# One kernel, seven small moves in its hand-written order: the first job in two token halves, weight sums on another engine, earlier preparation, expert weights in smaller parts

## The chip, the core and the metric

The kernel runs on one core of a Trainium2 chip. The metric is the time on the device in microseconds (us), lower is better. The core has five engines that matter here: TensorE (PE in the profile) for matrix products, VectorE (DVE) and GpSimd (POOL) for elementwise work, ScalarE (ACT) for activations and for copies out of the matmul banks, and SyncE (SP), which issues most DMAs. Each engine runs its own instructions in program order and waits for others by semaphores.

## What is computed

8192 tokens of 512 features, fp32. Cut to what matters:

```python
xn = layernorm(x)
h, f, i = split(xn @ W1 + b1, 3)              # 512 -> 3 x 1024
# gates from f and i in log space, value from h, then a scan along the sequence
hidden = scan(coefficient(f, i), value(h), init_h)
s = hidden @ W2 + b2                           # 1024 -> 512
shared = (silu(xn @ gate) * (xn @ up)) @ down  # 512 -> 1024 -> 512
e = argmax(xn @ gate_w)                        # one of 32 experts per token
routed = swiglu_e(xn * sigmoid(max logit))     # 512 -> 1024 -> 512, weights of expert e
out = x + s * silu(shared + routed)
```

## The kernel before

**Two halves.** The first half (up to about 2820 us) walks over the tokens in 16 chunks of 512 and does the recurrence and the shared expert. The second walks over the 32 routed experts: it gathers each expert's tokens by a table, multiplies, and adds the result to what the first half left in DRAM.

**Jobs and slots.** A chunk has 20 jobs, each one pair of 128-column blocks of one weight (h, f, i of the recurrence, g and u of the shared expert), 512 features by 256 columns. A job has 7 slots, a chunk 140 (`SC`). The loop over slots at the end of the file emits, for each slot, one piece of TensorE's work and then whatever was registered for this slot with `at(slot, function, ...)`. Nothing reorders it: the order in which the program is written is the order on every engine, so each `at` is a place in the queues of the engines that the function uses. What waits in a queue holds up all that stands behind it there.

**Chunk 0 and the others.** Chunk 0 multiplies plainly (`plain`, L641): per job two blocks of four accumulating matmuls of 128x512, evicted by ACT at the last (L661, L663) from three rotating banks `b`. Chunks 1 to 15 use a seven-product scheme (`multiply`, L665): each job has products P1 to P7 of 128x256, which need sums of weight blocks and of token blocks. The weight sums are made in chunk 0 (`combine`, L573: POOL L585 and L589, DVE L587 and L591), saved to DRAM and fetched later; the sums of token blocks (`t_sum`, L612, DVE L626) are made at the start of each chunk. The products' evicted parts are joined by additions (L720), on DVE or POOL.

**Preparation.** `Prep` loads a chunk's four token tiles, normalises them (L417), transposes them, makes the router's logits (L467 to L477), takes the largest (L485 to L497) and scales the tokens for the experts (`scale`, L506). `Prep.plan` places each of these steps in the chunk ahead of the one that it serves; for chunk 1 everything is shifted by 50 slots. Chunk 0's own preparation is the head of the program: four transposes per token tile on TensorE (L455), a copy each by ACT (L458), then the vector of biases (L1278) and the first job.

**Cells.** A `Cell` is the gate arithmetic of one pair of blocks: m = min(f, i, 0) on DVE (`low`, L758), f and i less m on POOL (`less`, L762), three exponentials on ACT (L766), f and i with m added on POOL (`weigh`, L771), their sum and its reciprocal on DVE (L775, L778, two halves), value, products (L792 to L782) and the scan (L804). Its steps stand at fixed slots behind the job of f, in `Cell.plan`.

**Projection.** The second products (W2, shared down) use the seven-product scheme too: `out_sum` (L878) makes four sums of weight blocks for each of the two, 128x1024 each (L886), and stores them to DRAM (`tdram`). `project_out` emits units of eight matmuls (L981), with weights `wP` that SP fetches in 512 KB tiles; in chunks 1 to 15 its units lie between the jobs' products, and the last chunk's units come at the end of the first half, alone.

**The table.** Each token's rank within its expert is counted chunk by chunk (`Dispatch.ranks`). After chunk 14, `places` computes on 32 partitions where each expert's tokens go: a chain of small DVE operations (L1099 to L1127) that ends in a matmul (`terms`, L1131). The token numbers are then written into a table in DRAM, merged, read back (`two`, `table`, `number`: L1239 to L1261), and turned into row addresses (`fours`, L1262), by which POOL gathers the tokens of the first experts (L205, L212) and their rows of the first half's results (`e_rest`, L222). The generator that makes the table does one part per slot; a bare `yield` in it lets a slot pass.

**The passage to the experts.** While the last units run, SP also fetches expert 0's weights: gate ahead of the loop, up in its 6th step, down in its 26th, 2 MB each (`weight`, L186).

Of the kernel before, what the change touches and what calls it, by code (L numbers as in the profile page):

```python
# [8 lines left out]
FP = mybir.dt.float32  # L9
# [8 lines left out]
P = 128  # L18
T = 512
# [14 lines left out]
def tile_kernel(  # L34
# [135 lines left out]
    class Chunk:  # L170
# [12 lines left out]
                (t, min(P, width - t * P)) for t in range(-(-width // P))  # L183
            ]

        def weight(self, tag):  # L186
            q = "gud".index(tag)
            w = self.alloc_w([P, KH * I], f"{self.name}_w{tag}")
            w = w.rearrange("p (k f) -> p k f", k=(KH, KH, NI)[q])
            self.src = self.src or self.w_src()  # L190
            rows = "(k p) f -> p k f" if tag == "d" else "(p k) f -> p k f"
            nc.sync.dma_start(out=w, in_=self.src[q].rearrange(rows, p=P))
            self.wt.append(w)

        def weights(self):
            for tag in "gud":
# [178 lines left out]
    def at(slot, what, *args):  # L375
        assert slot >= now
        steps.setdefault(slot, []).append(lambda: what(*args))
# [3 lines left out]
    class Prep:  # L381
# [126 lines left out]

        def plan(self, g):

            g += 50 if self.c == 1 else 0
            for t in range(NT):
                at(g + 2 + 2 * t, self.load, t)
                at(g + 16 + 2 * t, self.stats, t)
                at(g + 32 + 2 * t, self.normal, t)
                at(g + 35 + 2 * t, self.store, t)
                at(g + 43 + 2 * t, self.pieces, t)
                at(g + 50 + 2 * t, self.turn, t)
                at(g + 72 + 2 * t, self.again, t)
                at(g + 86 + t, self.scale, t)  # L520
            at(g + 12, self.keep)
            at(g + 24, self.variance, 0, NT)
            at(g + 28, self.spread, 0, NT)
            at(g + 66, self.router)
            at(g + 72, self.logits)
            at(g + 76, self.choose)
            at(g + 80, self.score)
# [113 lines left out]
    def bias(n, block):  # L641
        p, kind = JOBS[n % JC]
        col = "hfi".index(kind) * NJ + 2 * p + block
        return vec[:, col : col + 1]

    def plain(n, s):

        kind = JOBS[n % JC][1]
        for m in (s, s + 1) if s == 6 else (s,):
            block, k = divmod(m, KH)  # L650
            if k == 0:
                banks[n, block] = ps_b.tile([P, 512], FP, tag="b", name=f"b{block}_{n}")
            ps = banks[n, block]
            nc.tensor.matmul(
                ps, lhsT=natural[n][:, k, block * P : (block + 1) * P], rhs=xnTs[0][:, k, :],
                start=(k == 0), stop=(k == KH - 1),
            )
            if k == KH - 1:
                o = outs[n] if block else out_of(n)
                if kind in "gu":  # L660
                    nc.scalar.copy(o[:, block, :], ps)  # L661
                else:
                    nc.scalar.activation(o[:, block, :], ps, AF.Identity, bias=bias(n, block))  # L663

    def multiply(name, n):  # L665

        c = n // JC
        kind = JOBS[n % JC][1]
        A11, A12, A21, A22 = blocks(n)
        S = sums.get(n)  # L670
        b = xnTs[c]

        def B(k, m):
            return b[:, k * KQ : (k + 1) * KQ, m * HT : (m + 1) * HT]

        lhs, rhs, bank = {
            "P1": lambda: (A11, B(0, 0), "b"),
            "P2": lambda: (A12, B(1, 0), "a"),
            "P3": lambda: (S[:, 3], B(1, 1), "c"),
            "P4": lambda: (A22, tsum[c, 4], "b"),  # L680
            "P5": lambda: (S[:, 0], tsum[c, 1], "c"),
            "P6": lambda: (S[:, 1], tsum[c, 2], "b"),
            "P7": lambda: (S[:, 2], tsum[c, 3], "b"),
        }[name]()
        new = name in ("P1", "P2", "P5")
        if new:
            if bank == "b":
                ps = ps_b.tile([P, 512], FP, tag="b", name=f"b{n}")
            else:
                ps = ps_x.tile([P, 512], FP, tag=f"x{(n + (bank == 'a')) % 2}", name=f"{bank}{n}")  # L690
            banks[n, bank] = ps
        ps = banks[n, bank][:, :HT]
        for k in range(KQ):
            nc.tensor.matmul(  # L694
                ps, lhsT=lhs[:, k, :], rhs=rhs[:, k, :],
                start=(new and k == 0), stop=(k == KQ - 1),

                skip_group_check=True,
            )

        def part(tag, bufs):
            o = jp.tile([P, HT], FP, tag=tag, name=f"{tag}{n}", bufs=bufs)
            outs[n, tag] = o
            return o

        def evict(o, block):
            if block is None or kind in "gu":
                nc.scalar.copy(o, ps)  # L708
            else:
                nc.scalar.activation(o, ps, AF.Identity, bias=bias(n, block))  # L710

        if name == "P1":
            out_of(n)
            evict(part("p1", 2), 0)
            return
        o = outs[n]

        def join(eng, out, *tags):
            l, r = (outs.pop((n, tag)) for tag in tags)
            at(now + 1, lambda: eng.tensor_tensor(out, l, r, ALU.add))  # L720

        if name == "P2":
            evict(part("a", 2), None)
            join(nc.vector, o[:, 0, :HT], "a", "p1")
        elif name == "P5":
            evict(part("p5", 2), None)
        elif name == "P6":
            evict(part("u2", 2), 0)
        elif name == "P3":
            evict(part("c", 2), None)  # L730
            join(nc.vector, o[:, 0, HT:], "c", "u2")
        elif name == "P7":
            evict(part("u3", 2), 1)
            join(nc.vector if c == NCHUNK - 1 else nc.gpsimd, o[:, 1, HT:], "u3", "p5")
        elif name == "P4":
            evict(o[:, 1, :HT], 1)
            natural.pop(n)
# [6 lines left out]
    class Cell:  # L744
# [66 lines left out]
        def plan(self):  # L811
            g = SC * self.c + 7 * JOBS.index((self.p, "f"))
            for slot, what, *args in (
                (24, self.low), (25, self.less, "f"), (25, self.less, "i"),
                (27, self.exp, "m"), (29, self.exp, "f"), (31, self.exp, "i"),
                (32, self.weigh, "f"), (33, self.weigh, "i"), (37, self.total),
                (38, self.invert, 0), (39, self.sigmoid), (40, self.positive),
                (41, self.invert, 1), (43, self.value), (44, self.weighed),
                (45, self.divide, "f"), (46, self.divide, "i"),
                (47, self.scan, 0), (48, self.scan, 1),  # L820
            ):
                at(g + slot, what, *args)

    class Hidden:
# [54 lines left out]
    def out_sum(half, q):  # L879
        B11, B12, B21, B22 = out_blks[half][:4]  # L880
        l, r = {
            1: lambda: (B12, B11), 3: lambda: (B22, B12),
            2: lambda: (B22, out_blks[half][4]), 4: lambda: (B21, out_blks[half][5]),
        }[q]()
        o = out_tile(f"ot{half}_{q}")
        nc.vector.tensor_tensor(o, l, r, ALU.subtract)  # L886
        if q in (1, 2):
            out_blks[half].append(o)
        d = tdram[half, q] = dram.tile([P, NP * HC], FP, name=f"tdram{half}_{q}")
        at(now + 3, lambda: nc.sync.dma_start(out=d[:, :], in_=o.rearrange("p q f -> p (q f)")))  # L890
# [121 lines left out]
    class Dispatch:  # L1012
# [69 lines left out]
        def places(self):  # L1082
# [42 lines left out]
                    terms[:, q * E : (q + 1) * E], of, by[:E, 0:1], None, ALU.mult  # L1125
                )
            nc.vector.tensor_copy(terms[:, 4 * E :], extra)  # L1127
            for _ in range(4):
                yield
            ps = work("terms")  # L1130
            nc.tensor.matmul(  # L1131
# [136 lines left out]
    for t in range(NT):  # L1268
        first.stats(t)
        first.variance(t, 1)  # L1270
        first.spread(t, 1)
        if t:
            first.normal(t - 1)
            first.transpose(t - 1)
    first.normal(NT - 1)
    first.transpose(NT - 1)
    vps = work("vps")
# [27 lines left out]
    def spread_out(gen):  # L1305
        if next(gen, gen) is not gen:
            at(now + 1, spread_out, gen)

    at(SC + 100, d.clear)
    for q in range(NCHUNK // GC - 1):  # L1310
        at(SC * (GC * (q + 1) - 2) + 94, lambda q=q: spread_out(d.ranks(q)))
    last = SC * (NCHUNK - 1)

    def table():
# [10 lines left out]
        for half in range(2):  # L1325
            at(max(end + 20, END + 4) + half, d.numbers, half)

    at(last - SC + 94, lambda: spread_out(table()))

    fill = project_out()  # L1330
    PER = len(UNIT) * NP * 2
# [42 lines left out]
    ps_w = ctx.enter_context(  # L1374
        tc.tile_pool(name="ps_w", bufs=4, space=PSUM, side="right", reuse_waits="tile")
    )
    chunks[0].weight("g")
    k = 0
    while filled < 2 * NCHUNK * PER:
        now += 1  # L1380
        for step in steps.pop(now, ()):
            step()
        while filled < due(now):
            next(fill)
            filled += 1
        k += 1
        if k in (6, 26):
            chunks[0].weight("ud"[k // 26])
    next(fill, None)
    while steps:  # L1390
        now += 1
# [93 lines left out]
```

## Time and profile before

| | |
|---|---|
| time, median of 3 runs | 4345.41 us (4343.04 to 4348.74) |
| the profiled execution | 4345.11 us |
| its span | 4343.3 us |
| instructions | 52,479 |
| DMA traffic | 889.58 MB, mean 205 GB/s |

The page divides the span into 40 slices (some 109 us each) and gives for each the busy share of every engine in tenths. Further views give, for an engine, the us that it waited for each releaser, and a timeline: start, duration, engine, line, operation, output and inputs with shapes, and in brackets the idle time ahead of it with what ended it. The costliest groups of the first half are the job products (L694: 618.9 us for `b<-t,sums` alone) and the projection's products (L981: 601.9 us); those of the second half are L261 and L272 (515 to 519 us each). The mean granted TensorE clock of the execution is 0.992.

### The profile page before, as it was taken

To read this page: it belongs to the slowest core of one execution; us is meant where nothing else is said; L and a number is where in the kernel's file an instruction comes from. 1 tells how busy PE (TensorE), PEld (TensorE's weight loads), DVE (VectorE), ACT (ScalarE), POOL (GpSimd) and SP (SyncE) were. 2 spreads that over 40 slices of the span, in tenths; PEclk is the share of its full clock that TensorE was granted. 3 is DMA by queue.
4 is the path that set the end of the run, shared out by engine and by line. 5 is a ranking of instruction groups with operands and counts; after the bars stand their busy time and mean duration, and the time that the engine had idled before them with its cause. 6 is when DMAs were issued, how large, how long until landed. Compare 5 with 4: busy or idle time off the path is not lost. (4 is left out here: it accounts for less than half of the span.)

```text
span 4343.3 us, 52479 instructions
## 1 busy us (share of the span) xinstructions
PE 4262.1 (98%) x19031; PEld 3560.0 (82%) x19031; DVE 2761.5 (64%) x3507; ACT 1661.3 (38%) x3319; POOL 1748.4 (40%) x1410
## 2 busy tenths in 40 slices
PE   8899999999999999999999999999999999999998
PEld 3488888888888888888888888866777788889998
DVE  6787877886977778778878788723334334343332
ACT  3355555555555555555555544401111111111111
POOL 4445444534453444445434536642222233332210
PEclk9999999999999999999999999999999999999999
DMA  7667676676666666766766655574555555565561
GB/s 245 204 213 225 213 222 208 207 230 206 212 213 223 219 209 209 224 202 214 223 217 214 209 187 169 183 255 165 185 185 183 177 213 201 197 230 204 205 230 63
DMA packets 459433, 889.58 MB, mean 205 GB/s; under 512 B 35167, under 2 KB 285823, under 8 KB 450980
## 3 DMA queue, kind: packets, MB, share of 16 engines
q1 hardware_dynamic: 431588, 796.22, 55.1%
q0 software_dynamic: 27584, 89.98, 6.5%
q8 instruction: 152, 2.49, 0.2%
q14 instruction: 109, 0.89, 0.1%
HBM read 787.64 MB, written 116.50 MB: 208 GB/s over the span
## 5 line engine op out<-in xcount | busy, mean ns | idle before, releaser
L694 PE MATMUL b<-t,sums 128*128 128x256 f32 x2400 | 618.9, 380 | 8.6 <-DVE t L626 6.3
L981 PE MATMUL u<-wP,s 128*128 128x256 f32 x2048 | 601.9, 381 | 2.4 <-DMA wP<-tdram 2.4
L261 PE MATMUL e_acc<-e_h,e_wd 128*128 128x296 f32 (+15 forms) x2048 | 515.4, 397 | 5.5 <-DVE e_h L280 5.5
L272 PE MATMUL e_g<-e_xsT,e_wg 128*128 128x296 f32 (+15 forms) x2048 | 518.7, 396 | 1.0 <-DVE e_xsT L242 1.0
L272 PE MATMUL e_u<-e_xsT,e_wu 128*128 128x296 f32 (+15 forms) x2048 | 518.0, 396 | 0.0
L694 PEld LDWEIGHTS b<-t,sums 128*128 128x128 f32 x2400 | 454.1, 190 | 75.4 <-issue 6.5
L212 POOL DMA_INDIRECT e_xs<-rec,fours x276 | 263.1, 953 | 553.3 <-DVE e_xsT L247 458.7
L261 PEld LDWEIGHTS e_acc<-e_h,e_wd 128*128 128x128 f32 x2048 | 390.0, 191 | 94.0 <-DVE e_h L280 6.1
L272 PEld LDWEIGHTS e_u<-e_xsT,e_wu 128*128 128x128 f32 x2048 | 389.0, 190 | 87.2
L272 PEld LDWEIGHTS e_g<-e_xsT,e_wg 128*128 128x128 f32 x2048 | 383.0, 190 | 81.9 <-DVE e_xsT L242 1.2
L981 PEld LDWEIGHTS u<-wP,s 128*128 128x128 f32 x2048 | 390.5, 191 | 57.8 <-issue 4.7
L778 DVE RECIPROCAL d<-d 128x512 f32<-128x512 f32 x128 | 427.8, 3344 | 1.6
L277 ACT ACTIVATE e_sig<-e_g 128x280 f32<-128x280 f32 (+15 forms) x256 | 102.6, 401 | 769.5 <-PE e_g L272 764.5
L279 DVE TENSOR_TENSOR e_sig<-e_sig,e_g 128x280 f32<-128x280 f32 (+15 forms) x256 | 112.1, 438 | 425.0 <-ACT e_sig L277 424.9
L762 POOL TENSOR_TENSOR f<-m,f 128x1024 f32<-128x1024 f32 x64 | 154.8, 2419 | 410.6 <-DVE m L758 321.7
L694 PE MATMUL c<-t,sums 128*128 128x256 f32 x1200 | 309.0, 380 | 6.4 <-DVE t L626 6.4
L694 PE MATMUL c<-xnT,sums 128*128 128x256 f32 x1200 | 310.1, 381 | 0.3
L694 PE MATMUL a<-xnT,nat 128*128 128x256 f32 x1200 | 309.7, 381 | 0.0
L694 PE MATMUL b<-xnT,nat 128*128 128x256 f32 x1200 | 308.0, 379 | 0.0
L694 PE MATMUL b<-t,nat 128*128 128x256 f32 x1200 | 308.0, 379 | 0.0
L694 PEld LDWEIGHTS c<-t,sums 128*128 128x128 f32 x1200 | 228.4, 190 | 37.9 <-DVE t L626 6.8
L694 PEld LDWEIGHTS c<-xnT,sums 128*128 128x128 f32 x1200 | 227.1, 190 | 37.1 <-ACT p L708 6.3
(237 smaller groups left out, 7185.8 us busy)
## 6 DMA issues: line engine op xcount, KB each, us to landing
sums<-sdram SPq DMA_DIRECT2D x300, 512.0 KB, 4.8
nat<-in_L_attn_W_dram SPq DMA_DIRECT2D x192, 512.0 KB, 4.4
wP<-tdram SPq DMA_DIRECT2D x128, 512.0 KB, 4.1
e_wg<-L_ffn_routed_gate_w_dram SPq DMA_DIRECT2D x32, 2048.0 KB, 15.5
e_wu<-n_L_ffn_routed_up_w_dram SPq DMA_DIRECT2D x32, 2048.0 KB, 8.2
e_wd<-L_ffn_routed_down_w_dram SPq DMA_DIRECT2D x32, 2048.0 KB, 13.7
nat<-L_ffn_shared_gate_w_dram SPq DMA_DIRECT2D x64, 512.0 KB, 4.6
nat<-n_L_ffn_shared_up_w_dram SPq DMA_DIRECT2D x64, 512.0 KB, 4.2
```

The source lines that it names most:

```text
L212: nc.gpsimd.indirect_dma_start(out=r[:, b, :], out_offset=None, in_=rec1.rearrange("n (a d) -> (n a) d", a=NA), in_offset=bass.IndirectOff ...
L261: nc.tensor.matmul(accs[m][:, :W], lhsT=wd[:, j, m * P : (m + 1) * P], rhs=h[:, :W], start=(j == 0), stop=(j == NI - 1),)
L272: nc.tensor.matmul(o[:, :W], lhsT=w[:, k, j * P : (j + 1) * P], rhs=xsT[:, k, :W], start=(k == 0), stop=(k == KH - 1),)
L277: nc.scalar.activation(sig[:, :W], g[:, :W], AF.Sigmoid)
L279: nc.vector.tensor_tensor(sig[:, :W], sig[:, :W], g[:, :W], ALU.mult)
L694: nc.tensor.matmul(ps, lhsT=lhs[:, k, :], rhs=rhs[:, k, :], start=(new and k == 0), stop=(k == KQ - 1),  skip_group_check=True,)
L762: nc.gpsimd.tensor_tensor(v, self.m, v, ALU.subtract)
L778: nc.vector.reciprocal(self.d[:, s, :], self.d[:, s, :])
L981: nc.tensor.matmul(ps[:, q, :], lhsT=lhs[:, q * P : (q + 1) * P], rhs=w[:, p, :],  start=(q == 0 and p == 0 and name in ("P1", "P2", "P5") ...
```

## The change

Seven edits, none of which changes what is computed:

1. `first_half` emits the first job's matmuls for the first 256 tokens (both blocks, eight of 128x256) after the second token tile's transposes and ahead of the third's; `plain` then does the second 256 tokens of that job only.
2. The eight subtractions of `out_sum` go from DVE to POOL.
3. Chunk 1's preparation stands 12 slots earlier (shift 38 rather than 50), and `scale` of every chunk four slots earlier.
4. In chunk 0, the steps of a cell in its slots 27 to 33 (the exponentials and the two additions of m) stand two slots later.
5. For the last jobs of chunk 14 (12 to 19) the join behind P2 goes from DVE to POOL.
6. The ranks, and with the last of them the table, begin 5 slots earlier; the table's generator lets 9 slots pass ahead of the `terms` matmul rather than 4.
7. Expert 0's weights are fetched in twelve parts of 512 KB, in every second step of the loop over the last units (four parts of gate, four of up, four of down), rather than in three DMAs of 2 MB.

```diff
@@ -183,14 +183,15 @@
                 (t, min(P, width - t * P)) for t in range(-(-width // P))
             ]
 
-        def weight(self, tag):
+        def weight(self, tag, part=slice(None)):
             q = "gud".index(tag)
-            w = self.alloc_w([P, KH * I], f"{self.name}_w{tag}")
-            w = w.rearrange("p (k f) -> p k f", k=(KH, KH, NI)[q])
+            if len(self.wt) == q:
+                w = self.alloc_w([P, KH * I], f"{self.name}_w{tag}")
+                self.wt.append(w.rearrange("p (k f) -> p k f", k=(KH, KH, NI)[q]))
             self.src = self.src or self.w_src()
             rows = "(k p) f -> p k f" if tag == "d" else "(p k) f -> p k f"
-            nc.sync.dma_start(out=w, in_=self.src[q].rearrange(rows, p=P))
-            self.wt.append(w)
+            src = self.src[q].rearrange(rows, p=P)
+            nc.sync.dma_start(out=self.wt[q][:, part, :], in_=src[:, part, :])
 
         def weights(self):
             for tag in "gud":
@@ -508,7 +509,7 @@
 
         def plan(self, g):
 
-            g += 50 if self.c == 1 else 0
+            g += 38 if self.c == 1 else 0
             for t in range(NT):
                 at(g + 2 + 2 * t, self.load, t)
                 at(g + 16 + 2 * t, self.stats, t)
@@ -517,7 +518,7 @@
                 at(g + 43 + 2 * t, self.pieces, t)
                 at(g + 50 + 2 * t, self.turn, t)
                 at(g + 72 + 2 * t, self.again, t)
-                at(g + 86 + t, self.scale, t)
+                at(g + 82 + t, self.scale, t)
             at(g + 12, self.keep)
             at(g + 24, self.variance, 0, NT)
             at(g + 28, self.spread, 0, NT)
@@ -648,12 +649,13 @@
         kind = JOBS[n % JC][1]
         for m in (s, s + 1) if s == 6 else (s,):
             block, k = divmod(m, KH)
-            if k == 0:
+            if k == 0 and n:
                 banks[n, block] = ps_b.tile([P, 512], FP, tag="b", name=f"b{block}_{n}")
             ps = banks[n, block]
+            part = slice(0 if n else HT, T)
             nc.tensor.matmul(
-                ps, lhsT=natural[n][:, k, block * P : (block + 1) * P], rhs=xnTs[0][:, k, :],
-                start=(k == 0), stop=(k == KH - 1),
+                ps[:, part], lhsT=natural[n][:, k, block * P : (block + 1) * P],
+                rhs=xnTs[0][:, k, part], start=(k == 0), stop=(k == KH - 1),
             )
             if k == KH - 1:
                 o = outs[n] if block else out_of(n)
@@ -661,6 +663,15 @@
                     nc.scalar.copy(o[:, block, :], ps)
                 else:
                     nc.scalar.activation(o[:, block, :], ps, AF.Identity, bias=bias(n, block))
+
+    def first_half():
+        for block in range(2):
+            ps = banks[0, block] = ps_b.tile([P, 512], FP, tag="b", name=f"b{block}_0")
+            for k in range(KH):
+                nc.tensor.matmul(
+                    ps[:, :HT], lhsT=natural[0][:, k, block * P : (block + 1) * P],
+                    rhs=xnTs[0][:, k, :HT], start=(k == 0), stop=(k == KH - 1),
+                )
 
     def multiply(name, n):
 
@@ -721,7 +732,9 @@
 
         if name == "P2":
             evict(part("a", 2), None)
-            join(nc.vector, o[:, 0, :HT], "a", "p1")
+
+            late = n // JC == NCHUNK - 2 and n % JC > 11
+            join(nc.gpsimd if late else nc.vector, o[:, 0, :HT], "a", "p1")
         elif name == "P5":
             evict(part("p5", 2), None)
         elif name == "P6":
@@ -819,6 +832,8 @@
                 (45, self.divide, "f"), (46, self.divide, "i"),
                 (47, self.scan, 0), (48, self.scan, 1),
             ):
+                if self.c == 0 and 26 < slot < 34:
+                    slot += 2
                 at(g + slot, what, *args)
 
     class Hidden:
@@ -883,7 +898,7 @@
             2: lambda: (B22, out_blks[half][4]), 4: lambda: (B21, out_blks[half][5]),
         }[q]()
         o = out_tile(f"ot{half}_{q}")
-        nc.vector.tensor_tensor(o, l, r, ALU.subtract)
+        nc.gpsimd.tensor_tensor(o, l, r, ALU.subtract)
         if q in (1, 2):
             out_blks[half].append(o)
         d = tdram[half, q] = dram.tile([P, NP * HC], FP, name=f"tdram{half}_{q}")
@@ -1125,7 +1140,7 @@
                     terms[:, q * E : (q + 1) * E], of, by[:E, 0:1], None, ALU.mult
                 )
             nc.vector.tensor_copy(terms[:, 4 * E :], extra)
-            for _ in range(4):
+            for _ in range(9):
                 yield
             ps = work("terms")
             nc.tensor.matmul(
@@ -1272,6 +1287,8 @@
         if t:
             first.normal(t - 1)
             first.transpose(t - 1)
+        if t == 2:
+            first_half()
     first.normal(NT - 1)
     first.transpose(NT - 1)
     vps = work("vps")
@@ -1308,7 +1325,7 @@
 
     at(SC + 100, d.clear)
     for q in range(NCHUNK // GC - 1):
-        at(SC * (GC * (q + 1) - 2) + 94, lambda q=q: spread_out(d.ranks(q)))
+        at(SC * (GC * (q + 1) - 2) + 89, lambda q=q: spread_out(d.ranks(q)))
     last = SC * (NCHUNK - 1)
 
     def table():
@@ -1325,7 +1342,7 @@
         for half in range(2):
             at(max(end + 20, END + 4) + half, d.numbers, half)
 
-    at(last - SC + 94, lambda: spread_out(table()))
+    at(last - SC + 89, lambda: spread_out(table()))
 
     fill = project_out()
     PER = len(UNIT) * NP * 2
@@ -1374,7 +1391,6 @@
     ps_w = ctx.enter_context(
         tc.tile_pool(name="ps_w", bufs=4, space=PSUM, side="right", reuse_waits="tile")
     )
-    chunks[0].weight("g")
     k = 0
     while filled < 2 * NCHUNK * PER:
         now += 1
@@ -1383,9 +1399,11 @@
         while filled < due(now):
             next(fill)
             filled += 1
+        if k % 2 == 0 and k < 24:
+            q, part = divmod(k // 2, 4)
+            part *= (1, 1, 2)[q]
+            chunks[0].weight("gud"[q], slice(part, part + (1, 1, 2)[q]))
         k += 1
-        if k in (6, 26):
-            chunks[0].weight("ud"[k // 26])
     next(fill, None)
     while steps:
         now += 1
```

## Prediction

> **What bounds it now.** I read the page first, then TensorE's waits, then the timelines of the engines around each wait. Times are of one profiled execution: 4345.1 us, of which the span is 4343.3; the runs shown have their median at 4345.4, so a sum made against the execution holds for the median to 0.3 us.
>
> ```profile
> PE 4262.1 (98%) x19031; PEld 3560.0 (82%) x19031; DVE 2761.5 (64%) x3507; ACT 1661.3 (38%) x3319; POOL 1748.4 (40%) x1410
> PE   8899999999999999999999999999999999999998
> PEclk9999999999999999999999999999999999999999
> ```
>
> TensorE is busy 98% of the span. No edit removes a matmul, so all that can be won is idle time and the slow clock behind it. The list of what TensorE waited for shows where:
>
> ```profile
> PE b L654 <- ACT u L661: 10.7, 2, 5.7
> PE terms L1131 <- DVE terms L1127: 6.5, 1, 6.5
> PE c L694 <- DVE t L626: 6.4, 1, 6.4
> PE b L694 <- DVE t L626: 6.3, 3, 3.8
> PE e_acc L261 <- DVE e_h L280: 5.5, 1, 5.5
> PE u L981 <- DMA wP<-L_ffn_shared_down_w_dram: 4.2, 1, 4.2
> PE lgp L467 <- DVE xnT L436: 3.7, 1, 3.7
> PE u L981 <- DMA wP<-tdram: 2.4, 1, 2.4
> ```
>
> Columns: waiting line, releaser, us in all, times, longest. By the timeline the waits are: chunk 0 at 81.1 (5.74), 102.3 (1.52), 124.7 (4.96), 152.8 (3.71); the start of chunk 1 at 186.7 (6.43), 192.4 (0.53), 200.3 (2.02); the table's terms at 2582.1 (6.49); chunk 15 at 2620.5 (3.79); the passage to the experts at 2815.5 (4.23), 2826.7 (2.40), 2848.3 (0.98), 2871.7 (5.52); with three small ones 51.8 us. After 2872 there is none, so nothing is to be had in the expert half.
>
> A long wait costs more than itself. Windows of the timeline (us, busy and count by engine, granted clock, DMA):
>
> ```profile
> 81.10:83.00 1.90, 1.86 (x2) 0.83 (x3) 1.87 (x5) 1.90 (x3) 0.00 (x0) 0.50 0.00 0
> 2582.05:2584.00 1.95, 1.95 (x7) 1.53 (x8) 0.18 (x1) 0.00 (x0) 0.00 (x0) 0.50 0.00 0
> ```
>
> Clock 0.50 lasts about 4 us behind a wait of 3.8 us or more (81.1 to 85.0, 2582.1 to 2586.0), which halves the work done: some 2 us each, seven times, 14 us. The upper bound of everything is 51.8 + 14 = 66 us.
>
> **VectorE against GpSimd.** The second thing to see is that the two hold one another up:
>
> ```profile
> 72.03 3.27 POOL L762 TENSOR_TENSOR f<-m,f 128x1024 f32<-128x1024 f32 x1 [2.63 <-DVE m L758]
> 73.01 3.37 DVE L782 TENSOR_TENSOR i<-i,d 128x1024 f32<-128x1024 f32 x1
> 81.14 19.67 PE L654 MATMUL b<-xnT,nat 128*128 128x512 f32 x40 [5.74 <-ACT u L661]
> ```
>
> POOL's subtraction takes 3.27 where it takes 2.35 with VectorE idle; VectorE's product, 1.21 elsewhere, takes 3.37. The wait at 81.14 is this chain's end: m on DVE, two subtractions on POOL to 78.57, exp m and exp f on ACT, and only then the eviction that frees TensorE's bank.
>
> **The change, part by part** (gain positive).
>
> *First job in halves.* Token tile 1 is in SBUF at 9.36 (ACT's copy, 8.77 + 0.59); the first matmul now starts at 12.91. So 16 matmul instructions of 128x256 can start at 9.4; at the cold 0.427 us they end at 16.2, warm from 13.9 on (as now, 4.4 us after the first) at 15.1. But the transposes of tiles 2 and 3 stand behind them on TensorE (now at 9.06), and from there to the vector transpose, two transposes and two copies, take 3.85 now. After 15.1 + 3.1 the other half, 12 instructions ahead of the router's matmul, lands at 20.6; now that is 20.48. Gain 0, from -2 to +1.
>
> *Chunk 0: the eight weight sums on POOL, exp two slots later, chunk 1's preparation 12 slots earlier.* A sum is 1.21 on DVE, 2.35 on POOL: DVE is relieved of 9.7 us, POOL gets 18.8. What counts is POOL's order. In the changed program two sums (2.35 each) and a job's 0.73 stand ahead of weigh f and weigh i of the first cell, and its less ops start 0.7 to 1.5 later: weigh i ends at 55.0 + 0.9 + 4.7 + 0.7 = 61.3. Behind it on DVE stand total, two reciprocals (3.34 each), value and the next cell's m: 70.7 becomes about 75.5, since one sum between them (1.2) is gone. The wait now at 81.14 then ends near 85.0: +4.8, less the exp f (0.96) that the eviction is now ahead of. The second cell: two sums again, weigh i at 95.5 instead of 89.6, the 102.3 wait ends near 108. Then it comes back: DVE idles for POOL or others now at 43 (4.30), 50 (6.15), 85 (5.23), 120, 127 (2.9 each), 160 (5.5), and the preparation of chunk 1 (normals, transposes, top-1, four scalings of 0.47) fills these holes rather than standing ahead of the token sums. The router wait (3.71) goes; the 124.7 wait ends near 128; the first token sum, bound by the reciprocals behind the last weigh, about 1.2 later than now; the third 0.8 earlier, because two scalings no longer precede it. Gain 0.8. Bounds: nothing comes back, -12 (6.3 and 5.9 both arrive at TensorE); all seven waits vanish, 24.9 + 3 x 2 = 31. I take the value by the rows of POOL's order, with -6 to +12 for the range.
>
> The Trainium skill, "GPSIMD Engine Reference", section "Engine selection", advises VectorE and not GpSimd for two-input elementwise work, about twice as slow. The rows' ratio agrees (2.35 to 1.21); by the rule alone the move would be a loss of 8 x 1.14 = 9 us, but it says nothing of which engine has idle time here.
>
> *Chunks 1 to 13.* Scalings four slots earlier, behind the score that they need; no wait is listed there now. 0.
>
> *Terms and chunk 15.* The table's chain on DVE runs from 2569.61 to 2581.90. Five of its operations on 32x1 or 32x32 take 2.0 to 2.3 us beside POOL's subtractions and additions (2567.05 to 2580.84), where their neighbours take 0.15 to 0.7. Five slots earlier (1.2 us each) it starts near 2564.5; most of it runs ahead of POOL and ends near 2568 to 2570, the eight joins moved to POOL (0.42 off DVE each) helping. The matmul keeps its slot, so the wait of 6.49 and its cold clock (2.4: 0.50 to 2586, 0.59 to 2588) go: 8.9. Behind it the last cell's m and weigh come 2.4 to 2.9 later; DVE's 6.31 idle us at 2582, in which it waited for the stalled TensorE, take that up, yet chunk 15's token sums, on a DVE without holes from 2588 on, give back about 1.4: 7.5. Bounds 3 (the sums give back all that DVE's hole gave) and 11 (the 3.79 at 2620 shrinks too).
>
> *Expert 0's weights in 512 KB parts.* The queue rows now:
>
> ```profile
> 2814.09 0.33 SPq L1254 DMA_DIRECT2D table<-two  x1
> 2828.22 3.79 SPq L1261 DMA_DIRECT2D number<-table  x8
> 2856.02 0.95 POOL L222 DMA_INDIRECT e_rest<-rec,idx  x1 [0.30 <-issue]
> 2866.12 0.69 DVE L297 TENSOR_TENSOR e_rest<-e_rest,b2b 128x512 f32<-128x512 f32 x1 [11.90 <-DMA e_rest<-rec,idx]
> ```
>
> 4 MB of expert weights stand ahead of the table's 93 KB (14.1 us to land) and of the wP tiles; in the changed order 3 MB do, spread, and wP's first two wait behind 0.5 and 1 MB rather than 2. The waits of 4.23 and 2.40 and a cold clock (2) can go. But the same bytes move, at 371 to 432 GB/s in these windows: about 466 would be needed to hide all, so some 6 of 8.6 remain as gain at the first expert's start. The table lands near 2818, so the gathers can start 8 us earlier; POOL's program order keeps part of that: an output join of the last unit (its matmuls end near 2831) stands second behind expert 1's first gather, and 23 gathers at 1.25 us follow before e_rest. That issue moves from 2856 to about 2861, while DVE has the e_rest addition ahead of the product that the 5.52 wait is for (2871.74). So that wait stays or grows, and e_acc starts 3 to 5 earlier. Gain 4, bounds 0 and 9. No row has expert weights in parts; the nearest is wP, 512 KB in 4.1 us median, 9.0 when queued.
>
> The skill's "DMA: Bandwidth & Descriptors", section "Rules for kernel authors", asks for at least 1 MiB per DMA and speaks against this part. By its measured table (341 GB/s at 1 MB, 425 at 16 MB) 6 MB would take 3.6 us longer, an estimate; the windows with 512 KB tiles among them show up to 432, so I count nothing.
>
> **Sum**: 0 + 0.8 + 0 + 7.5 + 4 = 12.3; 4345.1 - 12.3 = 4333.
>
> **Rivals.** *A, the waits mostly vanish* (4290 to 4324): chunk 0's holes on DVE take all, the passage hides wP and the gate on e_rest. 20 from chunk 0, 11 and 9: 40, to 4305. For it: most of DVE's time in chunk 0 is waiting; against: the chain m, less, weigh, total is what the waits end on, and POOL is in it. *B, slower: POOL's queue.* The sums ahead of weigh delay two cells by 6.3 and 5.9, nothing comes back, and e_rest's later issue eats the passage's gain: -12.2 - 2 for a cold restart, -5 at e_rest, +7.5: 4345.1 + 11.7 = 4357. It decides if weigh i of the first cell ends later than 61 and the wait at 124.7 doesn't shrink. *C, no change:* chunk 0 costs 6 to 8, terms give 7.5, the passage 0 to 4: 4337 to 4354, centre 4343. For it: two of the three gains hang on engines that stay in program order.
>
> **Chances.** Forecast (4324 to 4337) 0.50, A 0.16, C 0.26, B 0.08. About 0.2%, 8.7 us, is what a measurement can tell: faster 0.66, same 0.26, slower 0.08. The range 4310 to 4348 leaves out B and half of A, and holds chunk 0's -6 as well as its +12.
>
> **To look at in the changed profile.** terms should no longer wait; the router neither; the first two waits of chunk 0 should be near 85 and 108, with weigh i of the first cell ending near 61; the table's DMA lands near 2818, e_rest is issued near 2861, e_acc starts near 2867 less what was won before. I'm wrong if weigh i is not late (then A), or if chunk 1 starts more than 5 us later than now (then B or C).

## The result

The changed kernel takes 4346.23 us (median of 12 runs, 4344.56 to 4348.44) against 4345.05 us for the one before (12 runs beside it): a ratio of 1.0004, 95% interval 0.9995 to 1.0013. That is no change. The profiled execution has a span of 4345.3 us against 4343.3.

The page's busy line, after:

```profile
PE 4261.2 (98%) x19047; PEld 3561.2 (82%) x19047; DVE 2803.5 (65%) x3491; ACT 1662.5 (38%) x3319; POOL 1767.0 (41%) x1426
```

TensorE's waits, after (line, releaser, us in all, times, longest; the lines of the file have moved by 1 to 15):

```profile
PE b L656 <- ACT u L663: 12.0, 3, 8.0
PE e_acc L262 <- DVE e_h L281: 7.7, 1, 7.7
...
PE b L705 <- DVE t L627: 6.4, 4, 3.8
PE c L705 <- DVE t L627: 5.6, 1, 5.6
PE u L996 <- DMA wP<-tdram: 4.9, 2, 3.2
PE b L656 <- ACT i L665: 3.8, 1, 3.8
PE u L996 <- DMA wP<-L_ffn_shared_down_w_dram: 2.3, 1, 2.3
...
PE cps L1087 <- DVE prev L1078: 1.8, 1, 1.8
...
PE lgt L478 <- ACT lgT L473: 1.7, 1, 1.7
```

`terms` (6.5) and the router's `lgp` (3.7) are gone. In their place the evictions of chunk 0 (12.0 and 3.8 against 10.7 and 1.5), the first expert's down product (7.7 against 5.5), the wP tiles (7.2 against 6.6) and a new wait for the ranks (1.8) have come. Idle time went in two places and came back in four.

Since nearly all of the run is matmuls, the time at which the same matmul starts tells what each stretch won or lost. Five places serve for all kernels: A, chunk 1's first product with a token sum; B, its third wait of that kind; C, chunk 15's long one; D, the first expert's first gate product; E, its second down product. "time" is this kernel less the kernel before, from medians of the same chip; the ratio is of those runs.

| kernel | A | B | C | D | E | time | ratio (95%) |
|---|---|---|---|---|---|---|---|
| before | 186.7 | 200.3 | 2620.5 | 2848.3 | 2871.7 | | |
| changed | 193.0 | 205.1 | 2617.9 | 2849.2 | 2874.8 | +1.2 | 1.0004 (0.9995 to 1.0013) |
| e1 sums on VectorE | 185.3 | 197.3 | 2611.2 | 2844.1 | 2869.3 | -1.8 | 0.9994 (0.9985 to 1.0004) |
| e2 old preparation | 193.3 | 205.6 | 2618.5 | 2848.6 | 2874.8 | +4.8 | 1.0010 (1.0000 to 1.0019) |
| e3 whole weights | 192.3 | 204.3 | 2617.1 | 2843.4 | 2866.4 | -4.0 | 0.9991 (0.9981 to 1.0001) |
| e4 table alone | 186.2 | 199.8 | 2615.4 | 2843.3 | 2866.4 | -4.9 | 0.9988 (0.9978 to 0.9998) |
| e5 sums behind weigh | 189.5 | 201.6 | 2615.7 | | | -6.5 | 0.9999 (0.9987 to 1.0012) |
| e7 sums, weights back | 186.0 | 198.1 | 2611.9 | | | -10.9 | 0.9978 (0.9968 to 0.9987) |
| e8 table, rest on POOL | 187.1 | 200.7 | 2614.6 | | | -9.7 | 0.9982 (0.9973 to 0.9992) |
| e9 rest ahead | 192.1 | 204.1 | 2616.9 | 2847.3 | 2865.1 | -7.8 | 0.9984 (0.9975 to 0.9994) |
| f1 combined | 186.5 | 198.5 | 2613.8 | 2840.5 | 2859.6 | -1.2 | 0.9994 (0.9985 to 1.0003) |
| f2 parts alone | 186.8 | 200.4 | 2620.7 | 2851.9 | 2878.4 | +7.3 | 1.0015 (1.0006 to 1.0024) |
| f3 sums alone | 192.2 | 205.8 | 2626.2 | 2855.0 | 2879.0 | +5.6 | 1.0011 (1.0002 to 1.0020) |
| f4 f1, old preparation, exp | 187.8 | 200.2 | 2613.7 | 2841.6 | 2862.8 | -0.4 | 0.9995 (0.9986 to 1.0004) |

One warning for the rows e5 and e7 to e9, which ran together on one chip: there the kernel before itself took 4358.1 us, 14 more than elsewhere, and in the profiles of e7 and e8 TensorE, VectorE and ACT stand still together for some 10 us around 2855 to 2864 with no wait of the kernel named. Their times are not set against the others, and places D and E are left out where this shows.

In the row of e5 the time and the ratio do not agree, since three of its ten runs took 4364 to 4369 us and the others 4349 to 4353; neither is read.

Kernels whose programs are alike up to a place differ there too: at A before, e4, f2 and e8 have 186.2 to 187.1, and the changed kernel, e3 and e9 192.1 to 193.0; at C the spread of e1, e7 and f1 is 2.6 us. So differences of about 1 us early in the run, and of 2 to 3 us later, are not read from a single pair of profiles.

So the changed kernel lost 4.8 us up to B, won 7.4 from B to C (2420.2 to 2412.8), and lost 5.6 from C to E (251.3 to 256.9): 3.0 later at E, 2.0 at the end.

### The profile page after: what moved, and what is told of

The parts are those of the page before. It is cut to its first block, busy times and chain, and to the rows that moved or that the text cites. A ratio compares the mean times of both kernels' runs of the same rounds, so it can differ in the third digit from the quotient of the medians.

```text
span 4345.3 us, 52554 instructions
## 1 busy us (share of the span) xinstructions
PE 4261.2 (98%) x19047; PEld 3561.2 (82%) x19047; DVE 2803.5 (65%) x3491; ACT 1662.5 (38%) x3319; POOL 1767.0 (41%) x1426
```

## The experiments

### Chunk 0: the sums on POOL (e1, e5, f3) or the earlier preparation (e2)

In the changed kernel's timeline POOL does what its program order says:

```profile
53.78 2.37 POOL L901 TENSOR_TENSOR ot<-wo,wo 128x1024 f32<-128x1024 f32 x1
56.09 2.36 POOL L784 TENSOR_TENSOR f<-m,f 128x1024 f32<-128x1024 f32 x1
58.39 0.73 POOL L586 TENSOR_TENSOR sums<-nat 128x256 f32<-128x256 f32 x1
59.07 2.35 POOL L784 TENSOR_TENSOR i<-m,i 128x1024 f32<-128x1024 f32 x1
```

L784 is `weigh`, L901 a sum. The second weigh ends at 61.4, where it ended at 55.0 before. What then reaches TensorE:

```profile
84.73 2.07 PE L656 MATMUL b<-xnT,nat 128*128 128x512 f32 x2 [8.01 <-ACT u L663]
...
193.03 2.07 PE L705 MATMUL c<-t,sums 128*128 128x256 f32 x4 [5.57 <-DVE t L627]
```

**e1**, the sums back on VectorE:

```diff
-        nc.gpsimd.tensor_tensor(o, l, r, ALU.subtract)
+        nc.vector.tensor_tensor(o, l, r, ALU.subtract)
```

> The changed kernel with the eight weight sums back on VectorE, all else as changed. Four places of the timeline carry the comparison: chunk 1's first wait for a token sum ends at 186.7 before and 193.0 changed; chunk 15's third such wait at 2620.5 and 2617.9; the first expert's first gate product at 2848.3 and 2849.2; its waited-for down product at 2871.7 and 2874.8. Theory Q (the sums on POOL stand ahead of weigh and delay two cells): weigh i of the first cell ends near 56 rather than 61.4, chunk 1's wait ends at 186 to 188, and 5 to 7 us are won over the changed kernel: 4339 to 4341. Rival R (the preparation 12 slots earlier puts its transposes and its top-1 ahead of the cells' work on VectorE, and so the delay stays): chunk 1's wait ends at 191 to 194 and the time is within 2 us of the changed kernel's 4346.

Measured: the second weigh ends at 54.6, place A is at 185.3.

```profile
52.23 2.33 POOL L784 TENSOR_TENSOR i<-m,i 128x1024 f32<-128x1024 f32 x1
```

Q holds: 7.7 us at A belong to this one line. At E 5.5 of them are left. The time is 1.8 under before, where the changed kernel is 1.2 over: 3.0, with two chips' references between.

**e2**, the preparation back:

```diff
-            g += 38 if self.c == 1 else 0
+            g += 50 if self.c == 1 else 0
```

> The changed kernel with chunk 1's preparation at its old slots (shift 50), the sums still on POOL. Theory Q: the two cells are as late as in the changed kernel (first two long waits ending near 85 and 110) and chunk 1's wait ends at 193 or later, since the router's 3.7 us wait may return: time 4346 to 4350. Rival R: the third and fourth cell get their time back, chunk 1's wait ends at 187 to 189, time 4340 to 4342.

Measured: A at 193.3, with the router's wait back (5.65 at 158.4): R falls. The router's wait is not worth its length: in the changed kernel, where it is gone, a wait that e2 does not have stands a little later in its place.

```profile
172.97 13.62 PE L656 MATMUL b<-xnT,nat 128*128 128x512 f32 x24 [3.25 <-ACT u L663]
```

The time, each against the kernel before on its own chip, is 3.6 over the changed kernel's; the medians themselves differ by 2.2 us. None of the five places shows it (E is the same), and the profiled execution of e2 is its fastest: where that comes from stays open.

**f3**, the sums alone in the kernel before (the diff of e1 the other way round):

> The kernel before with only the eight weight sums moved to POOL. Theory Q: chunk 1's first token-sum wait ends at 192 to 195 against 186.7, and the 6 to 8 us stay to the end: slower than before by that. Rival (the delay comes only together with the later exponentials or the earlier preparation): at 187 to 189, time within 2 us of before.

Measured: A at 192.2, 5.5 later, 7.2 later at E, time +5.6. The edit costs by itself, and by B (205.8) as much as the changed kernel loses there (205.1).

**e5**, the sums on POOL, but behind weigh:

```diff
-            at(b + 5 * k, out_sum, half, q)
+            at(b + 5 * k + (9 if k > 1 else 0), out_sum, half, q)
```

> The changed kernel, sums still on POOL, but the third and fourth sum of each weight nine slots later, so that they stand behind both cells' weigh in POOL's order instead of ahead of it; the amount of work on POOL is the same. Theory Q (only the place in the queue costs): weigh i of the first cell ends at 55 to 57 (61.4 as changed), chunk 1's first token-sum wait ends at 185 to 188 (193.0 as changed, 185.3 with the sums on VectorE), time 3 to 5 us under the changed kernel. Rival V (18.8 us more of work on POOL hold up VectorE wherever they stand): chunk 1's wait ends at 190 to 193, time as changed.

Measured: the second weigh ends at 56.9, and yet A is at 189.5. The place in the queue is worth 3.5 (193.0 to 189.5); the other 4.2 (189.5 to 185.3) remain with the sums on POOL at their new place: Q and V share it. The evictions still come late (84.3 and 106.6), behind the cells' next steps. At the new place the sums hold VectorE up elsewhere: two small casts, which take 0.26 and 0.11 us in e1, stand beside them.

```profile
57.15 2.40 DVE L132 CAST iot<-iot_i 128x186 f32<-128x186 int32 x1 [7.69 <-POOL iot_i L131]
65.08 2.05 DVE L132 CAST thr<-thr_i 128x21 f32<-128x21 int32 x1
```

Whether a place can be found at which the sums cost nothing is not shown.

### The table alone (e4)

```diff
-        at(SC * (GC * (q + 1) - 2) + 94, lambda q=q: spread_out(d.ranks(q)))
+        at(SC * (GC * (q + 1) - 2) + 89, lambda q=q: spread_out(d.ranks(q)))
-    at(last - SC + 94, lambda: spread_out(table()))
+    at(last - SC + 89, lambda: spread_out(table()))
-            for _ in range(4):
+            for _ in range(9):
```

> The kernel before with only the ranks and the table 5 slots earlier and 9 slots ahead of the terms product. Theory U (the terms wait and its slow clock are the gain of the change, and later stages keep it): no wait for terms, chunk 15's third token-sum wait ends at 2612 to 2614 rather than 2620.5, down product near 2864 to 2866, time 4337 to 4340. Rival T (the passage takes it back): chunk 15 as in U, down product at 2870 to 2872, time 4343 to 4345.

Measured: no wait for terms; C 5.1 earlier, E 5.3 earlier, time 4.9 less. U holds, though smaller: a new wait of 2.0 us for the ranks (cps) came in, which none of the theories had. The 5 us stay: the passage does not take them back.

### Expert 0's weights (e3, f2, e9)

In the changed kernel the queues read:

```profile
2826.16 5.67 SPq L1276 DMA_DIRECT2D number<-table  x8
...
2866.48 0.94 POOL L223 DMA_INDIRECT e_rest<-rec,idx  x1 [0.30 <-issue]
...
2873.58 0.69 DVE L298 TENSOR_TENSOR e_rest<-e_rest,b2b 128x512 f32<-128x512 f32 x1 [14.51 <-DMA e_rest<-rec,idx]
2874.19 0.54 DVE L281 TENSOR_TENSOR e_h<-e_sig,e_u 128x376 f32<-128x376 f32 x1
```

The table's numbers are read 2.1 us earlier than before, e_rest is gathered 10.5 later (2856.0 before), behind 24 gathers of other experts rather than 18; the addition of the bias waits for it on VectorE, and e_h, which TensorE needs, waits behind that addition.

**e3**, whole weights in the changed kernel:

```diff
+    chunks[0].weight("g")
     k = 0
...
-        if k % 2 == 0 and k < 24:
-            q, part = divmod(k // 2, 4)
-            part *= (1, 1, 2)[q]
-            chunks[0].weight("gud"[q], slice(part, part + (1, 1, 2)[q]))
         k += 1
+        if k in (6, 26):
+            chunks[0].weight("ud"[k // 26])
```

> The changed kernel with expert 0's weights in three DMAs of 2 MB at their old steps. Theory S (the parts cost: they spread 3 MB of weights among the tiles of the last units, and with them POOL's order has 24 rather than 18 gathers ahead of e_rest): up to chunk 15 as changed (2617.9), e_rest issued near 2855 rather than 2866, the waited-for down product at 2869 to 2871 rather than 2874.8, time 4341 to 4343. Rival T (the passage is paced by the bytes whatever their order, and takes back what arrives early): down product at 2872 to 2875, time 4344 to 4347.

Measured: D at 2843.4 and E at 2866.4, 8.4 earlier than as changed, with e_rest issued at 2853.1:

```profile
2866.41 4.13 PE L262 MATMUL e_acc<-e_h,e_wd 128*128 128x376 f32 x6 [5.05 <-DVE e_h L281]
```

S holds, and more is behind it than POOL's order: 5.7 of the 8.4 are there at D already.

**f2**, the parts alone in the kernel before (the diff of e3 the other way round, with the new `weight`):

> The kernel before with only expert 0's weights in twelve parts. Theory S (the parts cost in themselves): up to chunk 15 as before (third token-sum wait ends at 2620.5), the first gate product 3 to 6 us later than before (2851 to 2854 against 2848.3), e_rest issued behind 24 gathers at 2865 or later, the second down product at 2876 to 2879 against 2871.7, time 4 to 7 us over the kernel before. Rival T (only the earlier arrival of the changed kernel brought the passage to its limit of bytes): gate product at 2848 to 2849, down product within 2 us of before, same time.

Measured: up to C as before, then D +3.7, E +6.6, time +7.3. The parts cost by themselves, and all that the changed kernel loses behind C: from C to E f2 takes 257.7 us, the changed kernel 256.9, the kernel before 251.3.

**e9**, the parts, with the first expert's e_rest ahead of the other experts' tokens:

```diff
-            chunk.gather_rest()
-            if e == 0:
-                chunks[1].gather_in()
+            if e:
+                chunk.gather_rest()
+            else:
+                with tc.manual_schedule():
+                    chunk.gather_rest()
+                    chunks[1].gather_in()
```

> The changed kernel, weights in parts, with the gathers of the first expert's e_rest written out ahead of the 24 gathers of experts 1 to 3 on POOL. Theory S1 (the parts cost partly by POOL's order: e_rest is issued at 2866.5 as changed): issue at 2848 to 2853, the first gate product unchanged near 2849, the waited-for down product at 2867 to 2870 instead of 2874.8, time 4339 to 4342. Rival S2 (the rows land late because of the bytes of expert 1's weights, wherever the gather stands): down product at 2872 or later, time as changed, 4345 to 4347.

Measured: D at 2847.3; e_rest issued as soon as its rows are in DRAM; no wait at E (2865.1).

```profile
2850.89 1.00 POOL L223 DMA_INDIRECT e_rest<-rec,idx  x1 [16.33 <-DMA rec<-o]
```

S1 holds for the wait at E: POOL's order made it. What D lost is not touched by it.

### Together (e7, f1, f4), and one that did not tell (e8)

**e7** takes back both edits, e1's and e3's diffs:

> The changed kernel with both edits taken back that cost in the runs so far: sums on VectorE, expert 0's weights in three DMAs. Theory Q with S (the two losses are separate and add up): chunk 1's wait ends near 185, chunk 15's third token-sum wait near 2610 (2617.9 as changed), the waited-for down product at 2859 to 2861 (2874.8 as changed; 2869.3 and 2866.4 with one of the two), time 0.15 to 0.25% under the kernel before, 4333 to 4337. Rival T (the passage takes back what arrives early): down product at 2863 to 2866, time 4338 to 4341.

Measured: A and C as expected (186.0 and 2611.9). The passage can't be read (the warning above). Its ratio is the best of all, but its reference is the disturbed one.

**e8** adds to e4 a bias addition on POOL for the first expert:

```diff
-            nc.vector.tensor_tensor(r[:n, H : 2 * H], r[:n, H : 2 * H], b2b[:n, :], ALU.add)
+            eng = nc.gpsimd if name == "e0" else nc.vector
+            eng.tensor_tensor(r[:n, H : 2 * H], r[:n, H : 2 * H], b2b[:n, :], ALU.add)
```

> The kernel before with the table 5 slots earlier and, new, the bias addition to the first expert's gathered rows (e_rest) on POOL instead of VectorE. Theory W (the 5.1 to 7.7 us wait at the first down product is only VectorE's order: the addition, which waits for a gather, stands ahead of the product that TensorE needs): no wait there, the down product at 2861 to 2862 (2866.4 with the table alone), 5 us less than the table alone: 4332 to 4335. Rival X (another release is late right behind: down weights or tokens): 2865 or later, time 4337 to 4340.

Measured: C at 2614.6 as in e4; E has a wait of 8.96 inside the stretch in which all engines stand. Inconclusive.

**f1**, e7 with e9's order:

> What the runs so far recommend, in one kernel: the changed kernel with the sums on VectorE, expert 0's weights in three DMAs, and the first expert's e_rest gathered ahead of experts 1 to 3. Theory (the three effects are separate places and add up): chunk 1's first token-sum wait ends near 185 to 186 (186.7 before), chunk 15's third near 2611 (2620.5 before), the first gate product near 2838 (2848.3 before), no long wait at the second down product, which starts near 2856 (2871.7 before); time 13 to 16 us under the kernel before. Rival (the first expert then waits for something else, its down weights or its rows, or the expert half takes it back): second down product at 2862 or later, 6 to 10 us under the kernel before.

Measured: A at 186.5, C at 2613.8, D at 2840.5, E at 2859.6, 12.2 ahead of before, and the time only 1.2 less. The effects add up as far as E; from there on the rival's second half, that the experts take it back, came true and more. The timeline shows with what:

```profile
2859.56 2.79 PE L262 MATMUL e_acc<-e_h,e_wd 128*128 128x376 f32 x8 [1.13 <-DVE e_h L281]
...
2874.24 4.54 PE L262 MATMUL e_acc<-e_h,e_wd 128*128 128x376 f32 x8 [6.83 <-DVE e_h L281]
...
2887.18 4.49 PE L262 MATMUL e_acc<-e_h,e_wd 128*128 128x376 f32 x8 [3.35 <-DVE e_h L281]
```

and on VectorE:

```profile
2872.90 0.85 DVE L248 STREAM_TRANSPOSE e_xsT<-e_xs 128x384 f32<-128x384 f32 x1 [2.72 <-DMA e_xs<-rec,fours]
2873.68 0.50 DVE L281 TENSOR_TENSOR e_h<-e_sig,e_u 128x376 f32<-128x376 f32 x1
...
2885.95 0.72 DVE L298 TENSOR_TENSOR e_rest<-e_rest,b2b 128x512 f32<-128x512 f32 x1 [11.31 <-DMA e_rest<-rec,idx]
2886.59 0.53 DVE L281 TENSOR_TENSOR e_h<-e_sig,e_u 128x376 f32<-128x376 f32 x1
```

With e_rest first, expert 1's tokens come later, and their transposes (L248) stand ahead of the next e_h; two products on, expert 1's own e_rest does. The wait was not removed but handed on: 1.13 + 6.83 + 3.35 in place of 5.52, with stretches of half clock behind the two long ones. The lead over the kernel before is 12.2 us at E and 8.2, 2.8 and 1.0 at the next three down products. The same is seen in e9, which has no wait at E and one of 2.18 at 2893.0.

**f4**, f1 with chunk 1's preparation and chunk 0's exponentials at their old slots:

> The combined kernel with chunk 1's preparation and chunk 0's exponentials back at their slots of before. Theory (these two edits bring the 1.4 to 2.9 us by which chunk 1 was ahead of before once the sums were back on VectorE): chunk 1's first token-sum wait ends near 186.7 and its third near 200 (185.3 and 197.3 with both edits), 2 to 3 us over the combined kernel. Rival (the first job in halves brought it, or they only look like it): within 1 us of the combined kernel at both places.

Measured: A at 187.8, B at 200.2, 1.4 and 1.7 behind f1; time 0.7 more, which a measurement can't tell. These two edits do bring about 1.5 us locally (A is 185.3 to 186.5 in the three kernels that have them and no sums on POOL).

Of all runs, the table alone (e4) is the clearest gain: 4.9 us, ratio 0.9988 (0.9978 to 0.9998), against the changed kernel's 1.0004. The lead of the changed kernel without its two costly edits (e7) was not measured on an undisturbed chip. The first job in halves, the scalings four slots earlier and the joins on POOL were not run alone.

## Why the prediction was right and wrong

The range, 4310 to 4348, holds the 4346, by its width of 38 us and not by the working: 12.3 us of gain were forecast, none is there, and the likeliest case did not come. What came is close to rival C in size, and not in its make-up: C let chunk 0 cost 6 to 8 (4.8 up to B), the terms give 7.5 (7.4) and the passage give 0 to 4 (it cost 5.6). The sign that was named for B or C, chunk 1 more than 5 us late, did come (6.3 at A). Of B's condition one half came: the first weigh ends later than 61, but the wait at 124.7 shrank, to 0.79.

- **The bound** was right: TensorE is busy 4261.2 us for 4262.1 and idle 84.1 for 81.2, and the expert half behind E is the same to 1.0 us (3.0 later at E, 2.0 at the end). That nothing can be had there holds for time lost, not for time won: f1's lead went there.
- **The head**, 0 forecast: the first half of the job ran from 9.28 to 15.96, and the matmuls behind the router start at 25.61 instead of 25.45. Right.
- **Chunk 0**, +0.8 forecast, -4.8 measured. The working up to the evictions held (second weigh 61.4 for 61.3, the next cell's m at 75.4 for 75.5, the two waits ending at 84.7 for 85.0 and 110.1 for 108), but for a new wait of 1.13 at 99.2. The step that failed is "Then it comes back". The third cell's m is 7.3 late (122.7 for 115.4), the fourth's 5.9 (165.2 for 159.4), and the wait that was to end near 128 ends at 130.8. VectorE had holes, but ahead of each late step, and its chain from the third cell's sum (137.3) to 160 has none: a delay goes straight through it, and holes that lie in the wait for the late thing itself can't make it up. e2 shows that the preparation's place did neither harm nor good there. The third cell's m, before and after:

```profile
115.41 1.21 DVE L758 SCALAR_TENSOR_TENSOR m<-f,i 128x1024 f32<-128x1024 f32 x1
...
122.71 1.74 DVE L771 SCALAR_TENSOR_TENSOR m<-f,i 128x1024 f32<-128x1024 f32 x1
```

- **The terms**, 7.5 forecast, 7.4 measured from B to C. The mechanism held: the table's chain on VectorE takes 3.4 us (2567.75 to 2571.16) instead of 12.3, and the wait for it is gone. (Three of its operations, not five, had taken 2.0 to 2.3 us.) That the size is so near is in part luck. A new wait of 1.75 to 2.0 us for the ranks, which I had not seen, takes some of the gain back, and the half clock that follows it in e1, e4, e5, e7, e8, f1 and f4, worth 1.7 us there, did not follow it in the changed kernel. The joins moved to POOL are not needed for it: e8, which has e4's program up to C, wins 6.3 from B to C, as do e1 (6.3) and e7 (6.4), which have the joins. e4 wins 4.6 there, with half clock from 200.8 to 204.3, right behind B, which costs it 1.7.
- **The passage**, +4 forecast, -5.6 measured. Three steps failed. "4 MB stand ahead of the table, in the changed order 3 MB do", from which the table was to land near 2818: the count holds, but the table's DMA, issued at 2813.8, took 12.4 us where it took 14.1, the numbers were read 2.1 us earlier, and the two halves of fours begin at 2832.5 and 2833.3 instead of 2831.6 and 2833.9. The DMA engines are full from 2810 to 2830 (99% and more, 370 to 418 GB/s in stretches of 5 us), and the bytes ahead do not give the time by themselves: with the same bytes whole or in parts, D differs by 3.7 us (f2 and before) and by 5.7 (e3 and changed). "The waits of 4.23 and 2.40 can go": two waits became four (1.45, 1.65, 3.23, 2.32), as weights and tiles now came side by side. Why the parts make those tiles late by so much is not shown. And e_rest was issued at 2866.5, not 2861, behind 24 gathers and a join that itself came later (2836.3 for 2831).

The Trainium skill had spoken against two edits, and both verdicts proved right here. "GPSIMD Engine Reference", section "Engine selection", prefers VectorE for such elementwise work: f3 measures 5.6 us for the move, less than the 9 that its ratio gave. "DMA: Bandwidth & Descriptors", section "Rules for kernel authors", asks for DMAs of 1 MiB or more: f2 measures 7.3 us for the smaller ones, though no run shows a lower rate; what the profiles show to have changed is the order in which the transfers come.

## What to carry to other kernels

An engine with 60% idle time is not free: what counts is which step of a chain stands behind the moved work in its queue, and whether the idle time lies ahead of that step or after it. Where transfers fill the DMA engines, splitting one changes who is late, and can cost (7.3 us in f2): counting the bytes ahead did not foretell it. Look, too, at what the scheduler does to the queues of other engines. A wait at one instruction of an engine that works in order is removed only if nothing behind it waits for data of the same age: f1 won 12 us at one matmul, and three of that kind later 1.0 was left.

## What the runs showed of the hardware that I had not expected

A wait need not be long to be followed by the slow clock, and the same wait is not always followed by it. The granted clock in the 3.2 us behind each wait, over all fourteen profiles (the stretches in which all engines stand left out): behind waits of 3.5 us or more it was 0.50 to 0.69 each time. Of fifteen waits of 3.20 to 3.44 us ten had 0.50 to 0.66 behind them and five 1.00 (3.24 in e3 and 3.44 in e8 among them). Shorter ones went either way: 2.32 (changed) gave 0.50 and 2.40 (before) 0.52, 2.44 (f4) and 2.72 (e4) 1.00. The wait for the ranks, at the same place in several kernels, gave 0.58 behind 1.75 us (f1), 0.70 behind 1.75 (e1) and 1.00 behind 1.76 (changed). "TensorE: Matmul & The Clock Gate", section "What's actually happening", puts the slow clock behind an idle window of about 3.4 us that runs free of the program; a free-running window agrees with the scatter, the half clock behind 1.75 us does not agree with a whole idle window.
